# Two ends of a 32-group pipeline: the last group's graphs taken apart, and the setup put ahead of everything

## The chip, the cores and the metric

The kernel runs on one core of a Trainium2 chip. The metric is the device time of one execution in microseconds; lower is better. The core has five engines that run side by side and wait for each other through semaphores: TensorE (PE, matrix products and transposes into PSUM; PEld is its loading of weights), VectorE (DVE), ScalarE (ACT), GpSimd (POOL) and SyncE (SP, which here only issues transfers). ScalarE can issue transfers too, in its own order with its other work.

## What is computed

64 graphs of 256 nodes with 256 features each pass four layers. Each layer is attention over the neighbours that the adjacency matrix allows, a residual and a normalisation.

```python
def reference(x, adj, ...):
    # layer 0: 4 heads, projections Wq Wk Wv Wo, its own layer norm inside
    x = _layernorm(x + _L0_gnn_ref(x, adj, L0_gnn_Wq, ...))
    # layer 1: 8 heads, q = k = v = layer_norm(x); then an MLP
    #          x + gelu(y @ W1 + b1) @ W2 + b2        (256 -> 1024 -> 256)
    x = _layernorm(x + _L1_gnn_ref(x, adj, ..., L1_gnn_W1, L1_gnn_b1, L1_gnn_W2, L1_gnn_b2))
    # layer 2: one head, e[i,j] = leaky_relu(s1[i] + s2[j]), Wh = x @ W
    x = _layernorm(x + _L2_gnn_ref(x, adj, L2_gnn_W, L2_gnn_a))
    # layer 3: one head, scores x * a0 @ x^T, leaky_relu, softmax
    x = _layernorm(x + _L3_gnn_ref(x, adj, ...))
    return x                                          # (64, 256, 256) float32
```

(cut and abridged.)

## The kernel before

Two graphs make a group (G = 2), 512 tokens in four blocks of 128 (TB = 4; QB = 2 blocks per graph). There are 32 groups. Each group is a generator; at each `yield` the others go on, so that the instructions of up to three groups are interleaved. Group 0 begins at step 0, the next one every 15 steps (PACE). TensorE's instructions keep the order in which the program names them.

First the loads, most of them through SyncE:

```python
    setup = act.tile([P, NF, T], F32, name="setup", tag="hT", bufs=1)...   # scratch in hT's place
    first = load_group(0)                                   # x and adj, through SyncE
    wqT = load_rows("L0_gnn_WqT", D, nc.scalar)             # through ScalarE: these four alone
    wkT = load_rows("L0_gnn_WkT", D, nc.scalar)
    bq = load_column(a["L0_gnn_bq"], D, "bq", nc.scalar)
    bk = load_column(a["L0_gnn_bk"], D, "bk", nc.scalar)
    wvT = load_rows("L0_gnn_WvT", D)                        # through SyncE: the rest
    woT = load_rows("L0_gnn_WoT", D)
    ...                                                     # bv, bo, wx, a12, beta0, gamma0, ..., a0
    second = load_group(1)
    w1 = load_rows("L1_gnn_W1", DFF)
    w2 = load_rows("L1_gnn_W2", D)
```

Then the layers. The parts that matter here (cut):

```python
    def project(dst, srcT, w, extra, row=None):
        chunks = w.shape[1]
        for i in range(G):
            pm = ps_m.tile([P, QB, D], F32, name="pm")
            for q in range(QB):
                t = i * QB + q
                for c in range(chunks):
                    matmul(pm[:, q, :], srcT[:, c, t * P:(t + 1) * P], w[:, c, :], ...)
                if row is not None:
                    matmul(pm[:, q, :], onesb, row, start=False, stop=True)
                if chunks > NC:
                    yield
            ...                                             # add the residual

    def layer1(xb, z, mask):
        ...                                                 # attention
        hT = act.tile([P, NF, T], F32, name="hT", bufs=1)
        ...                                                 # W1 and gelu into hT
        yield from project(x2, hT, w2, both, b2m)           # the MLP's second product
        return (yield from renormed(x2))

    def renormed(y, var=None):
        xn = act.tile([P, TB, W], F32, name="xn")
        for i in range(G):
            mv, rstd = stats(y, i)                          # DVE statistics, GpSimd's power
            scaled(xn, y, i, mv, rstd[:, 0])                # DVE
        ...
        return xn

    def values_of(e, v, one, x, rs, var=None):              # e^T v, divided, plus x, renormed
        ...

    def layer2(x, mask):
        xT = transposed(x)                                  # 8 transposes, 2 ScalarE copies
        ...                                                 # wh = x W in 4 blocks, ScalarE copies
        nc.scalar.activation(ex, wh[:, :, D:D + 3], AF.Exp)
        ...                                                 # 4 transposes of ex, 4 DVE products into e
        nc.vector.tensor_tensor(e..., e..., mask..., ALU.mult)
        return (yield from values_of(e, wh, D + 3, x, ...))

    def layer3(g, x, mask):
        for c in range(NC):
            pt = to_psum(x, c)
            nc.scalar.copy(xT[:, c, :], pt)
            nc.scalar.activation(xa[:, c, :], pt, AF.Identity, scale=a0[:, c:c + 1])
        ...                                                 # ps = xT^T xa, 8 products
        nc.scalar.activation(e, ps, AF.Exp, bias=shift)
        nc.scalar.activation(low, ps, AF.Exp, bias=shift, scale=SLOPE)
        nc.vector.tensor_tensor(e, e, low, ALU.max)
        nc.vector.tensor_tensor(e..., e..., mask..., ALU.mult)
        return (yield from values_of(e, x, D, x, r_3[:, g], last[:, g]))

    def group(g):
        x, adj = (first, second)[g] if g < 2 else load_group(g)
        yield
        adjb = io.tile([P, TB, N], BF16, name="adjb", bufs=1)             # one buffer for all groups
        nc.scalar.activation(adjb, adj, AF.Copy, accum_out=there[:, g:g + 1])
        nc.scalar.activation(adj.bitcast(F32), adj, AF.Square, ...)
        yield
        ...                                                 # 8 transposes of adjb, mask on DVE from both
        xb, z = yield from layer0(g, x, mask)
        x = yield from layer1(xb, z, mask)
        x = yield from layer2(x, mask)
        x = yield from layer3(g, x, mask)
        nc.sync.dma_start(out[g * G:(g + 1) * G]..., x[:, :, 0:D])
```

The setup's arithmetic is a generator of its own, `prepare`, whose parts come from step 5 on, between the steps of group 0: `bop` (bo plus bv Wo), three extra columns of `wx` (from L2's W and a), `b2m` (b2 minus beta1 as three bf16 rows, each written by a small transfer from DVE's `part`), and `bounds` (from wsum, the product `ones` x `wsum` on PE and a GpSimd power), which the final flag reads.

Of the kernel before, what the change touches and what calls it, by code (L numbers as in the profile page):

```python
# [8 lines left out]
F32 = mybir.dt.float32  # L9
# [7 lines left out]
P = 128  # L17
N = 256
# [19 lines left out]
PREPARE = 5  # L38
# [357 lines left out]
def usual_input(ctx: ExitStack, tc: tile.TileContext, a: dict, out: bass.AP, flag: bass.AP):  # L396
# [52 lines left out]
    def load_rows(name, cols, queue=nc.sync):  # L449

        src = a[name]
        t = const.tile([P, src.shape[0] // P, cols], F32, name=name)
        queue.dma_start(t, src.rearrange("(c p) f -> p c f", p=P))
        return t

    def load_column(src, n, name, queue=nc.sync):

        t = const.tile([P, n // P], F32, name=name)
        queue.dma_start(t, src.rearrange("(c p) -> p c", p=P))
        return t  # L460

    setup = act.tile([P, NF, T], F32, name="setup", tag="hT", bufs=1).rearrange("p f t -> p (f t)")

    def load_all(src, name, at=None):

        t = const.tile([P, D], F32, name=name) if at is None else setup[:, at:at + D]
        nc.sync.dma_start(t, src.unsqueeze(0).to_broadcast([P, D]))
        return t


    first = load_group(0)
    wqT = load_rows("L0_gnn_WqT", D, nc.scalar)
    wkT = load_rows("L0_gnn_WkT", D, nc.scalar)
    bq = load_column(a["L0_gnn_bq"], D, "bq", nc.scalar)
    bk = load_column(a["L0_gnn_bk"], D, "bk", nc.scalar)
    wvT = load_rows("L0_gnn_WvT", D)
    woT = load_rows("L0_gnn_WoT", D)
    bv = load_column(a["L0_gnn_bv"], D, "bv")
    bo = load_all(a["L0_gnn_bo"], "bo", 0)

    wx = const.tile([P, NC, D + 3], F32, name="wx")
    nc.sync.dma_start(wx[:, :, 0:D], a["L2_gnn_W"].rearrange("(c p) f -> p c f", p=P))
    a12 = setup[:, 768:1280].rearrange("p (s d) -> p s d", s=2)
    nc.sync.dma_start(a12, a["L2_gnn_a"].rearrange("(s f) o -> o s f", s=2).to_broadcast([P, 2, D]))
    beta0 = load_all(a["L0_gnn_beta"], "beta0")
    gamma0 = load_all(a["L0_gnn_gamma"], "gamma0")
    beta1r = load_all(a["L1_gnn_beta1"], "beta1r")
    gamma1r = load_all(a["L1_gnn_gamma1"], "gamma1r", 256)
    b2 = load_all(a["L1_gnn_b2"], "b2", 512)
    gamma1 = load_column(a["L1_gnn_gamma1"], D, "gamma1")  # L490
    beta1 = load_column(a["L1_gnn_beta1"], D, "beta1")
    gamma2 = load_column(a["L1_gnn_gamma2"], D, "gamma2")
    beta2 = load_column(a["L1_gnn_beta2"], D, "beta2")
    b1 = load_column(a["L1_gnn_b1"], DFF, "b1")
    a0 = load_column(a["L3_gnn_a0"], D, "a0")
    second = load_group(1)
    w1 = load_rows("L1_gnn_W1", DFF)
    w2 = load_rows("L1_gnn_W2", D)

    wa1 = const.tile([P, 2, NC], F32, name="wa1")  # L500
    b2m = const.tile([P, D], BF16, name="b2m")
    onesb = const.tile([P, P], BF16, name="onesb")
    bop = const.tile([P, D], F32, name="bop")
    bounds = const.tile([P, 2], F32, name="bounds")

# [49 lines left out]
    def to_psum(src, c):  # L555

        pt = ps_m.tile([P, T], F32, name="pm")
        for t in range(TB):
            transpose(pt[:, t * P:(t + 1) * P], src[:, t, c * P:(c + 1) * P], ident)
        return pt  # L560

    def transposed(src, scale=None, bias=None):

        dst = act.tile([P, NC, T], F32, name="xT")
        for c in range(NC):
            pt = to_psum(src, c)
            if scale is None:
                nc.scalar.copy(dst[:, c, :], pt)
            else:
                nc.scalar.activation(dst[:, c, :], pt, AF.Identity, bias=bias[:, c:c + 1], scale=scale[:, c:c + 1])  # L570
        return dst
# [109 lines left out]
    def project(dst, srcT, w, extra, row=None):  # L681
# [3 lines left out]
        for i in range(G):  # L685
# [76 lines left out]
    def layer1(xb, z, mask):  # L762
# [34 lines left out]
        yield from project(x2, hT, w2, both, b2m)  # L797
        return (yield from renormed(x2))

    def renormed(y, var=None):  # L800
# [3 lines left out]
        for i in range(G):  # L804
            mv, rstd = stats(y, i)
            if var is not None:
                nc.gpsimd.tensor_copy(var[:, i * QB:(i + 1) * QB], mv[:, :, 1])
            scaled(xn, y, i, mv, rstd[:, 0])
# [4 lines left out]
    def values_of(e, v, one, x, rs, var=None):  # L813

        y = act.tile([P, TB, D], F32, name="y")
        for t in range(TB):
# [9 lines left out]
        return (yield from renormed(y, var))  # L826

    def layer2(x, mask):
        xT = transposed(x)
# [5 lines left out]
        for tb in range(TB):  # L835
# [9 lines left out]
        nc.scalar.activation(ex, wh[:, :, D:D + 3], AF.Exp)  # L845
        pt = ps_m.tile([P, G, N], F32, name="pm")
        for t in range(TB):
            transpose(pt[:, t // QB, t % QB * P:(t % QB + 1) * P], ex[:, t, 0:1].to_broadcast([P, P]), ident)
        e = act.tile([P, G, QB, N], F32, name="qT")
        for t in range(TB):  # L850
            i, kc = divmod(t, QB)
            nc.vector.tensor_scalar(e[:, i, kc, :], pt[:, i, :], ex[:, t, 1:2], ex[:, t, 2:3], ALU.mult, ALU.max)
        nc.vector.tensor_tensor(e.rearrange("p g k q -> p (g k q)"), e.rearrange("p g k q -> p (g k q)"),  # L853
                                mask.rearrange("p g k -> p (g k)"), ALU.mult)
        yield
        return (yield from values_of(e, wh, D + 3, x, small.tile([P, TB], F32, name="r")))

    def layer3(g, x, mask):
        xT = act.tile([P, NC, T], F32, name="xT")
        xa = act.tile([P, NC, T], F32, name="z")  # L860
        for c in range(NC):
            pt = to_psum(x, c)
            nc.scalar.copy(xT[:, c, :], pt)
            nc.scalar.activation(xa[:, c, :], pt, AF.Identity, scale=a0[:, c:c + 1])
        yield
        ps = ps_s.tile([P, G, QB, N], F32, name="ps")
        for i in range(G):
            for kc in range(QB):
                for c in range(NC):
# [5 lines left out]
        nc.scalar.activation(e, ps, AF.Exp, bias=shift)  # L875
        nc.scalar.activation(low, ps, AF.Exp, bias=shift, scale=SLOPE)  # L876
        nc.vector.tensor_tensor(e, e, low, ALU.max)  # L877
        nc.vector.tensor_tensor(e.rearrange("p g k q -> p (g k q)"), e.rearrange("p g k q -> p (g k q)"),
                                mask.rearrange("p g k -> p (g k)"), ALU.mult)
        yield  # L880
        yield from rest("e3")
        return (yield from values_of(e, x, D, x, r_3[:, g], last[:, g]))

    def group(g):
        x, adj = (first, second)[g] if g < 2 else load_group(g)
# [18 lines left out]
        x = yield from layer1(xb, z, mask)  # L904
        x = yield from layer2(x, mask)
        x = yield from layer3(g, x, mask)
        nc.sync.dma_start(out[g * G:(g + 1) * G].rearrange("b (q p) d -> p (b q) d", p=P), x[:, :, 0:D])

    def prepare():


        bvr = setup[:, 2560:2816].rearrange("p (c q) -> p c q", c=NC)
        nc.vector.tensor_copy(bvr, bv.unsqueeze(2).to_broadcast([P, NC, P]))
        pm = ps_m.tile([P, D], F32, name="pm")
        for c in range(NC):
            matmul(pm, bvr[:, c, :], woT[:, c, :], start=c == 0, stop=c == NC - 1)
        nc.vector.tensor_tensor(bop, pm, bo, ALU.add)

        yield
        wa = setup[:, 1280:2304].rearrange("p (s c d) -> p s c d", s=2, c=NC)  # L920
        for s in range(2):
            nc.vector.tensor_tensor(wa[:, s], wx[:, :, 0:D], a12[:, s:s + 1, :].to_broadcast([P, NC, D]), ALU.mult)
        nc.vector.tensor_reduce(wa1, wa, AX.X, ALU.add)
        for k, (s, share) in enumerate(((0, SLOPE - 1.0), (1, SLOPE), (1, 1.0))):
            nc.vector.tensor_scalar(wx[:, :, D + k:D + k + 1], wa1[:, s, :].unsqueeze(2), share, None, ALU.mult)

        yield

        nc.gpsimd.memset(onesb, 0.0)
        nc.gpsimd.memset(onesb[0:3, :], 1.0)  # L930
        nc.gpsimd.memset(b2m, 0.0)
        left = setup[:, 2304:2560]
        nc.vector.tensor_tensor(left, b2, beta1r, ALU.subtract)
        part = setup[:, 3328:3456].bitcast(BF16)
        for k in range(3):
            nc.vector.tensor_copy(part, left)
            nc.sync.dma_start(b2m[k:k + 1, :], part[0:1, :])
            if k < 2:
                nc.vector.tensor_tensor(left, left, part, ALU.subtract)

        yield

        sq = setup[:, 2816:3328].rearrange("p (s d) -> p s d", s=2)
        nc.vector.tensor_tensor(sq[:, 0], gamma1r, gamma1r, ALU.mult)
        nc.vector.tensor_tensor(sq[:, 1], beta1r, beta1r, ALU.mult)
        lengths = const.tile([P, 4], F32, name="lengths")
        nc.vector.tensor_reduce(lengths[:, 0:1], sq[:, 0], AX.X, ALU.max)
        nc.vector.tensor_reduce(lengths[:, 1:2], sq[:, 1], AX.X, ALU.add)
        wsq = const.tile([P, 2, NC], F32, name="wsq")
        nc.vector.tensor_tensor(wsq, wa1, wa1, ALU.mult)  # L950
        wsum = const.tile([P, 2], F32, name="wsum")
        nc.vector.tensor_reduce(wsum, wsq, AX.X, ALU.add)
        pm = ps_m.tile([P, 2], F32, name="pm")
        matmul(pm, ones, wsum, start=True, stop=True)
        nc.vector.tensor_copy(lengths[:, 2:4], pm)
# [16 lines left out]
    while waiting or running:  # L972
# [8 lines left out]
        if step >= PREPARE:  # L981
            next(preparing, END)
# [54 lines left out]
```

## Time and profile before

| | before |
|---|---|
| time, median of 3 (lowest, highest) | 2766.12 us (2765.04, 2766.6) |
| span of the profiled execution | 2764.3 us |
| PE busy | 2678.1 us (97%) |
| DVE busy | 1932.5 us (70%) |
| ACT busy | 1294.7 us (47%) |
| POOL busy | 576.8 us (21%) |
| first product or transpose on PE | 10.85 us |
| transfers in the first 35 us | 7.63 MB |
| last normalisation ends | 2756.64 us |

The profile is one execution seen by the hardware profiler. It gives for every engine when each instruction ran and what ended the wait before it. In its lines, L521 and L524 are the helpers through which all of the groups' products and transposes go, so that tiles, not lines, tell them apart: `pm<-v,qT` is a product into PSUM tile pm from v and qT. "x16" is the number of instructions (a float32 product runs as two passes, so 8 products give 16). The granted PE clock is a share of full speed.

### The profile page before, as it was taken

Reading aid. Unit: us, or ns where it says so; the run is one execution under the profiler, and the core shown is the slowest. Engines: PE = TensorE matmul, PEld = TensorE weight load, DVE = VectorE, ACT = ScalarE, POOL = GpSimd, SP = SyncE. Lnnn points to the kernel's source line nnn. Section 1 sums busy time; section 2 is a strip of 40 time slices with the busy share of each in tenths; the row PEclk is TensorE's granted clock in tenths of the full one; section 3 lists DMA queues with packets and bytes.
Section 4 is the critical chain, followed back from the end, with each engine's and each line's share of the span. In section 5 each row is a group of like instructions: output and inputs, shape, how many; then the busy total and the mean of one; then the engine's idle time right before and its main releaser. Section 6 shows DMA issues by size and latency. Waiting matters only on the chain.

```text
span 2764.3 us, 45617 instructions
## 1 busy us (share of the span) xinstructions
PE 2678.1 (97%) x17288; PEld 1842.3 (67%) x17288; DVE 1932.5 (70%) x6346; ACT 1294.7 (47%) x1953; POOL 576.8 (21%) x1138
## 2 busy tenths in 40 slices
PE   6999999999999999999999999999999999999986
PEld 3666666666666767666667666666666666666664
DVE  5667776777676777766777767677767776767754
ACT  3444544544544444544445445445444445444441
POOL 1112121221221221212221222222212212222211
PEclk8999999999999999999999999999999999999998
DMA  4000000000000000000000000000000000000000
GB/s 126 16 8 24 16 24 16 24 16 16 24 21 19 16 24 16 24 16 24 16 24 16 24 16 24 16 20 20 24 16 17 23 16 24 9 16 9 9 8 16
DMA packets 57904, 57.78 MB, mean 21 GB/s; under 512 B 5072, under 2 KB 57296, under 8 KB 57680
## 3 DMA queue, kind: packets, MB, share of 16 engines
q1 hardware_dynamic: 56592, 54.28, 6.4%
q8 instruction: 139, 2.28, 0.3%
q14 instruction: 85, 0.70, 0.1%
q10 hardware_dynamic: 1088, 0.53, 0.1%
HBM read 38.02 MB, written 16.78 MB: 20 GB/s over the span
## 4 chain that ended last, share of the span: by engine, by line
PE 68%; DVE 20%; POOL 8%; issue 2%; ACT 1%; DMA 1%; POOLq 0%; SPq 0%; ACTq 0%; DVEq 0%
PE pm L521 53%; PE ps L521 9%; PE pm L524 6%; POOL rstd L544 6%; DVE xn L552 4%; DVE e L597 3%; DVE st L537 3%; POOL ve L540 2%; DVE z L552 1%; DVE e L591 1%; DVE mv L538 1%; ACT e L589 1%; DVE y L750 1%; DVE xb L756 1%; DVE xb L552 1%
## 5 line engine op out<-in xcount | busy, mean ns | idle before, releaser
L589 ACT ACTIVATE e<-ps 128x1024 f32<-128x1024 f32 x384 | 372.2, 1021 | 356.5 <-PE ps L521 353.3
L521 PE MATMUL pm<-L_gnn_W,hT 128*128 128x256 f32 x2048 | 463.2, 379 | 0.0
L521 PE MATMUL pm<-xT,L_gnn_W 128*128 128x512 f32 x1024 | 450.6, 593 | 0.0
L521 PEld LDWEIGHTS pm<-L_gnn_W,hT 128*128 128x128 f32 x2048 | 383.9, 190 | 63.2 <-issue 15.1
L597 DVE SCALAR_TENSOR_TENSOR e<-e,mask 128x256 f32<-128x256 f32 x1024 | 399.3, 454 | 29.1 <-ACT e L589 29.1
L794 ACT ACTIVATE hT<-pm,b 128x512 f32<-128x512 f32 x256 | 175.9, 687 | 477.5 <-PE pm L521 477.5
L540 POOL TENSOR_SCALAR ve<-mv 128x2 f32<-128x2 f32 x384 | 93.1, 243 | 1315.5 <-DVE mv L538 1121.7
L521 PEld LDWEIGHTS pm<-xT,L_gnn_W 128*128 128x128 f32 x1024 | 192.5, 190 | 216.5 <-issue 214.2
L537 DVE BATCH_NORM_STATS2 st<-y 128x6 f32<-128x256 f32 x768 | 300.4, 410 | 5.6
L544 POOL TENSOR_TENSOR rstd<-ve,mhalf 128x2 f32<-128x2 f32 (+1 forms) x384 | 297.9, 776 | 26.6
L552 DVE TENSOR_SCALAR xn<-y,mv,rstd 128x256 f32<-128x256 f32 x384 | 163.5, 472 | 127.2 <-POOL rstd L544 127.2
L877 DVE TENSOR_TENSOR qT<-qT,kT 128x1024 f32<-128x1024 f32 x32 | 39.2, 1226 | 195.1 <-ACT kT L876 195.1
L521 PE MATMUL pm<-e,z 128*32 128x256 f32 x2048 | 149.2, 385 | 3.7 <-DVE e L597 2.9
L521 PE MATMUL pm<-e,v 128*32 128x256 f32 x2048 | 135.5, 382 | 16.9 <-DVE e L591 16.9
L591 DVE TENSOR_TENSOR e<-e,mask 128x1024 f32<-128x1024 f32 x128 | 148.3, 1220 | 0.5 <-ACT e L589 0.5
L521 PE MATMUL ps<-xT 32*128 32x256 f32 x2048 | 147.8, 402 | 0.0
L780 POOL TENSOR_TENSOR both<-y,xb 128x512 f32<-128x512 f32 x64 | 81.7, 1277 | 314.6 <-DVE y L779 314.6
L718 POOL TENSOR_TENSOR x<-x,beta 128x1024 f32<-128x1024 f32 x32 | 75.5, 2359 | 334.9 <-PE pm L524 334.9
L570 ACT ACTIVATE xT<-pm,beta,gamma 128x512 f32<-128x512 f32 x128 | 92.9, 773 | 103.9 <-PE pm L524 103.6
L521 PE MATMUL ps<-qT,kT 64*128 64x256 f32 x1024 | 128.0, 389 | 0.3 <-ACT e L589 0.3
L538 DVE BATCH_NORM_AGGREGATE mv<-st 128x2 f32<-128x6 f32 x768 | 121.6, 171 | 3.0
L521 PE MATMUL pm<-v,qT 128*128 128x260 f32 x512 | 120.3, 389 | 3.3 <-DVE qT L853 3.3
(144 smaller groups left out, 4321.1 us busy)
## 6 DMA issues: line engine op xcount, KB each, us to landing
x<-in_x SPq DMA_DIRECT2D x32, 512.0 KB, 3.8
adj<-in_adj SPq DMA_DIRECT2D x32, 512.0 KB, 3.8
out<-xn SPq DMA_DIRECT2D x32, 512.0 KB, 2.9
L_gnn_W<-in_L_gnn_W SPq DMA_DIRECT2D x2, 1024.0 KB, 8.6
L_gnn_WqT<-in_L_gnn_WqT ACTq DMA_DIRECT2D x1, 256.0 KB, 4.9
L_gnn_WkT<-in_L_gnn_WkT ACTq DMA_DIRECT2D x1, 256.0 KB, 6.8
L_gnn_WvT<-in_L_gnn_WvT SPq DMA_DIRECT2D x1, 256.0 KB, 7.5
L_gnn_WoT<-in_L_gnn_WoT SPq DMA_DIRECT2D x1, 256.0 KB, 7.8
```

Of the source, the lines that this page charges most:

```text
L521: in_order(nc.tensor.matmul(*args, **kw))
L524: in_order(nc.tensor.transpose(*args))
L537: nc.vector.bn_stats(st[:, q, :], src[:, t, 0:D])
L538: nc.vector.bn_aggr(mv[:, q, :], st[:, q, :])
L540: nc.gpsimd.tensor_scalar(ve[:, 0], mv[:, :, 1], EPS, None, ALU.add)
L544: nc.gpsimd.tensor_tensor(rstd, ve, mhalf[:, 0:k * QB].rearrange("p (k t) -> p k t", k=k), ALU.pow)
L552: nc.vector.tensor_scalar(dst[:, t, 0:D], src[:, t, 0:D], mv[:, q, 0:1], rstd[:, q:q + 1], ALU.subtract, ALU.mult)
L570: nc.scalar.activation(dst[:, c, :], pt, AF.Identity, bias=bias[:, c:c + 1], scale=scale[:, c:c + 1])
L589: nc.scalar.activation(e, ps, AF.Exp, scale=scale)
L591: nc.vector.tensor_tensor(e, e, mask.unsqueeze(1).to_broadcast([P, 2, QB * N]), ALU.mult)
L597: nc.vector.scalar_tensor_tensor(e[:, h, k], e[:, h, k], 1.0, mask[:, k], ALU.mult, ALU.mult, accum_out=sums[:, kc, c, j:j + 1])
L794: nc.scalar.activation(hT[:, f, :], pm, AF.Gelu, bias=b1[:, f:f + 1])
```

## The change

It has two parts. For the last group alone, from the MLP's second product on, the two graphs go separately: each is its own generator, the second one two turns behind the first, so that one graph's waits may be filled with the other's work. And the beginning has another form: all weights come through ScalarE, x and adj of the first groups through SyncE, and the setup's arithmetic stands ahead of the groups instead of between their steps.

```diff
-    first = load_group(0)
-    wqT = load_rows("L0_gnn_WqT", D, nc.scalar)
-    wkT = load_rows("L0_gnn_WkT", D, nc.scalar)
...
+    wqT = load_rows("L0_gnn_WqT", D)              # load_rows, load_column and load_all
+    wkT = load_rows("L0_gnn_WkT", D)              # all use nc.scalar.dma_start now
+    wvT = load_rows("L0_gnn_WvT", D)
+    woT = load_rows("L0_gnn_WoT", D)
...                                                # bq bk bv bo gamma0 beta0 gamma1 beta1 ...
+    w1 = load_rows("L1_gnn_W1", DFF)
+    b1 = load_column(a["L1_gnn_b1"], DFF, "b1")
+    w2 = load_rows("L1_gnn_W2", D)
+    b2 = load_all(a["L1_gnn_b2"], "b2", "xn")
+    wx = const.tile([P, NC, D + 3], F32, name="wx")
+    nc.scalar.dma_start(wx[:, :, 0:D], ...)
+    a12 = act.tile([P, 2, D], F32, name="a12", tag="z")
+    nc.scalar.dma_start(a12, ...)
+    for s in range(2):
+        nc.vector.tensor_tensor(wa[:, s], wx[:, :, 0:D], a12[:, s:s + 1, :]..., ALU.mult)
+    nc.vector.tensor_reduce(wa1, wa, AX.X, ALU.add)
...
+    for k in range(3):
+        nc.vector.tensor_copy(part, rest)
+        nc.sync.dma_start(b2m[k:k + 1, :], part[0:1, :])
...                                                # bop, squares, lengths, wsum
+    nc.tensor.matmul(pm, ones, wsum, start=True, stop=True)
+    nc.vector.tensor_copy(lengths[:, 2:4], pm)
+    nc.gpsimd.tensor_tensor(roots, lengths, half, ALU.pow)
...                                                # longest, bounds
-    def project(dst, srcT, w, extra, row=None):
+    def project(dst, srcT, w, extra, row=None, gs=ALL):
...                                                # the same gs in to_psum, transposed, renormed,
...                                                # values_of, layer2, layer3
     def group(g):
-        x, adj = (first, second)[g] if g < 2 else load_group(g)
+        x, adj = load_group(g)
...
-        x = yield from layer1(xb, z, mask)
-        x = yield from layer2(x, mask)
-        x = yield from layer3(g, x, mask)
-        nc.sync.dma_start(out[g * G:(g + 1) * G]..., x[:, :, 0:D])
-
-    def prepare():
...
+        y, hT, both = yield from layer1(xb, z, mask)
+
+        def others(gs):
+            yield from project(y, hT, w2, both, b2m, gs)
+            x = yield from renormed(y, gs)
+            x = yield from layer2(x, mask, gs)
+            x = yield from layer3(g, x, mask, gs)
+            i, j = g * G + gs[0], g * G + gs[-1] + 1
+            nc.sync.dma_start(out[i:j]..., x[:, gs[0] * QB:(gs[-1] + 1) * QB, 0:D])
+
+        if g < B // G - 1:
+            yield from others(ALL)
+            return
+
+        parts = [others((i,)) for i in ALL]
+        turn = 0
+        while parts:
+            for r in parts[:turn // QB + 1]:
+                if next(r, END) == END:
+                    parts.remove(r)
+            turn += 1
+            yield
```

(cut at "..."; comments in the diff are added here.)

## The prediction

> **What bounds the kernel now.** I read the page first, then the busy time by stretches, then the timeline of the two ends. The stretches (columns: busy time with instruction counts of PE, PEld, DVE, ACT and POOL; granted PE clock; DMA share; GB/s):
>
> ```profile
> 0.00:40.00 40.00, 27.09 (x194) 16.87 (x195) 18.22 (x44) 16.85 (x27) 5.07 (x19) 1.00 0.70 191
> 40.00:70.00 30.00, 15.78 (x92) 10.18 (x93) 20.62 (x72) 9.26 (x13) 7.35 (x11) 0.72 0.11 36
> 70.00:2660.00 2590.00, 2560.26 (x16711) 1761.08 (x16709) 1846.05 (x6095) 1244.28 (x1874) 549.24 (x1072) 1.00 0.06 18
> 2660.00:2712.00 52.00, 47.78 (x201) 34.43 (x202) 24.46 (x65) 17.12 (x26) 8.01 (x16) 0.97 0.03 11
> 2712.00:2764.00 52.00, 27.16 (x93) 19.76 (x91) 23.16 (x74) 7.14 (x13) 7.13 (x20) 0.76 0.06 22
> ```
>
> Between 70 and 2660 us PE is busy 99% of the time, at full clock. The compiled order of the changed kernel has the same instructions in the same order there on every engine, so that stretch is worth zero. What can change is when it starts (the first 70 us) and what follows it (the last 52 us, where PE is half idle). A later start moves everything behind it one for one, because a full PE can't catch up.
>
> The start of before, from the timeline (start, duration, engine, line, operation):
>
> ```profile
> 8.33 1.06 ACT L888 ACTIVATE adjb<-adj 128x1024 bf16<-128x1024 int32 x1 [3.87 <-DMA adj<-in_adj]
> 10.85 1.01 PE L524 MATMUL pm<-identb,adjb 128*128 128x128 bf16 x8 [10.85 <-ACT adj L889]
> 13.12 3.44 DVE L922 TENSOR_TENSOR setup<-wx,setup 128x512 f32<-128x512 f32 x2
> 13.60 0.59 ACT L568 COPY xT<-pm 128x512 f32<-128x512 f32 x1 [0.27 <-PE pm L524]
> 25.84 2.00 PE L521 MATMUL ps<-qT,kT 64*128 64x256 f32 x16
> 27.61 0.29 DVE L936 CAST setup<-setup 128x256 bf16<-128x256 f32 x1 [6.90 <-DMA b2m<-setup]
> ```
>
> The first group waits only for its own adjacency (landed at 8.3 us); the setup arithmetic fits into gaps. First scores start at 25.84 us, my reference point. All starting loads together keep the DMA engines busy to about 30 us.
>
> The end of before, from its timeline:
>
> ```profile
> 2723.59 6.51 PE L521 MATMUL pm<-v,qT 128*128 128x260 f32 x16 [3.33 <-DVE qT L853]
> 2736.26 5.37 PE L521 MATMUL ps<-z,xT 128*128 128x256 f32 x16 [0.41 <-ACT z L864]
> 2741.66 1.11 ACT L875 ACTIVATE qT<-ps,shift 128x1024 f32<-128x1024 f32 x1 [4.39 <-PE ps L521]
> 2746.45 5.29 PE L521 MATMUL pm<-xn,qT 128*128 128x257 f32 x16 [4.82 <-DVE qT L878]
> ```
>
> and the last normalisation in the chain of waits (start, duration, what):
>
> ```profile
> 2755.91 0.73 DVE xn L552 x2
> ```
>
> One dependent chain for both graphs: every stage waits for the one before, the engines take turns, and PE gets 0.76 of its clock. It ends with that normalisation at 2756.64; the rest to 2764.3 is the output's landing, the flag and the program's end.
>
> **What the Trainium skill says.** (1) "DMA: Bandwidth & Descriptors", section "Issuing engines are not separate DMA queues": transfers issued from SyncE and ScalarE share the same 16 DMA engines, and a second issuer only saves issue time. The trace agrees: with both issuing, the first 10 us moved 227 GB/s at a DMA share of 0.86. So the second queue doesn't shorten the loading. (2) "SBUF — State Buffer", section "SBUF: two separate sides", on the shared port pair: VectorE operations with two SBUF inputs and GpSimd operations lock each other out. The trace agrees: one of the two L922 products took 689 ns, the other 2835 ns, when GpSimd's 2.36 us addition ran at 13.65. The changed order has GpSimd idle there, so I count 0.69 us each. (3) "TensorE: Matmul & The Clock Gate", Part 1: an idle window of some 3.4 us halves PE's clock. The trace agrees at both ends (0.50 in 50 to 60 us, 0.66 in 2720 to 2740), but not for the first 10 us, idle at 1.00.
>
> **The change, part by part: the start.** In the compiled order, ScalarE issues 23 loads before its first activation; SyncE has only x and adj of the first two groups ahead of the b2m copies. VectorE does the whole setup before the first mask, and PE's second product of all is the one of wsum, ahead of the first transposes. So nothing of group 0 moves on PE before a12, the last large load, has landed and VectorE is through.
>
> *When a12 lands.* Before moved 7.63 MB by about 30 us. Up to a12 it is now 6.56 MB: four loads of 0.524, four weights of 0.262, W1 and W2 with 2.10, wx and a12 0.52, six broadcast rows 0.79. The 1.05 MB less (adj of groups 2 and 3) is 3 us at 350 GB/s, and some gaps between issues vanish: 26.5 us, within 24 to 29. ScalarE is past its last issue at about 18 us by my count of issue times (0.5 us each) and reused completion semaphores, so it isn't the last wait.
>
> *VectorE to wsum.* Durations of before: L922 2 x 0.69, bop 0.42, L923 1.21, cast 0.28, wx 0.29, rest 0.41, squares 2 x 0.41, lengths 2 x 0.40, wsq and wsum 0.30, sum 5.9: 32.4 us. The second cast needs the first b2m copy read; that took 8.7 us in before behind W1 and W2 on SyncE's queue. Now that queue is nearly empty, b2 lands ahead of wx and a12, and I expect no wait.
>
> *To the first scores.* wsum on PE 0.4, its copy 0.15 and hops: 33.3. GpSimd's roots 1.03: 34.4. Seven small VectorE operations 1.04: 35.5. The mask 1.23: 36.8. Only then group 1's adjb on ScalarE (there is one adjb buffer), 1.06 + 0.19: 38.1. In the compiled order the second xT copy of group 0 stands behind that: 0.59, so 38.7. In before that copy ended at 14.2 and the scores began 11.6 later; without bop's product between Q and K (0.87) that is 10.8. Scores at 49.5, that is 23.7 later. After that before lost about 1.3 us to setup operations standing ahead of score masks (mask 2 ready at 29, done at 31.2) which no longer occurs: 22.4. A cold PE after 30 idle us may cost some: I add 1. **Start: +23.4 us.**
>
> **The end.** The PE order of the changed kernel: graph 0's four transposes, its wx; graph 1's transposes, its wx; ex of 0, values of 0, ex of 1, values of 1; transposes and ps of 0, then of 1; last values of 0, then of 1. W2's products and group 30's last values keep their places, so the split begins to act at 2713.2. Halving durations of before:
> - wx of graph 0 starts at 2714.1 (before: 2715.1), graph 1's ends at 2719.0. VectorE is busy with group 30 to 2719.95, so graph 0's mask is done at 2721.6 (before, both: 2723.5).
> - Values of 0 at the slow clock, 3.2: 2724.8. Graph 1's ex stands behind them in PE's order; its mask is done at 2728.0, its values at 2731.3.
> - Transposes of 0 after that, ScalarE's four copies of 0.4: 2733.5; ps 2735.2; exponentials 2736.6; then the copies of graph 1, its ps at 2739.6.
> - Values of 0 2739.6 to 2742.2; graph 1's exponentials to 2741, its mask 2743.6, its values to 2746.4; y, statistics, GpSimd's 1.0, xn: 2750.0.
>
> Against 2756.65 that is 6.65 us. PE's strict order makes graph 1 wait behind graph 0 twice, which is why half-size stages don't bring more. **End: -6.7 us**, within -3 to -11.
>
> **Sum.** 2766.1 + 23.4 - 6.7 = 2782.8, rounded to 2783.
>
> **Rivals.** (a) The later start is hidden, as loads overlap with setup anyway. For: ScalarE's casts and the transfers do overlap. Against: PE did 27 us of work in the first 40 us, which now comes later, and the middle has 1% of slack. With the start lost only to 10 us the end's gain nearly covers it: about 2769. (b) The end gains more, because interleaving two graphs keeps PE warm. v, ps and last values take 6.5 + 5.4 + 5.3 us, against 3.6 to 3.7 each for the groups of 16 at full clock in the timeline near 2677, 2695 and 2709; warm throughout and without stalls the end would be 11 to 14 us shorter: about 2777. Against: gaps of 2 to 3 us remain in my schedule. (c) The first b2m copy queues behind the loads as in before (8.7 us): second cast only at 34 or later instead of 30, start +27: about 2787. Against: the queue is now another. (d) Waits for lanes of completion semaphores starve the DMA engines between 10 and 15 us, when small loads are alone: a12 at 29 to 30, about 2786.
>
> **Range and chances.** The start's error is mainly a12's landing (2.5 us to either side) and the clock; the end's some 3 us. Together some 7 us: 2775 to 2791. The two per cent are 55 us either way; neither end has so much to win or lose. Faster 0.01, same 0.97, slower 0.02.
>
> **What would show it.** First transposes on PE at 33 us, having waited for VectorE's wsum; the first L922-like product waiting for a12 at about 26.5; the two products 0.69 us each; first scores near 49.5; PE full again from about 93; from there to 2713 the same length as before; the last xn some 6.7 us sooner relative to group 30's last values. Wrong would be: first scores under 42 (a12 earlier, or the setup off the path), or a tail shorter by over 11 us or not at all.

## Result: where the changed kernel's time lies

| | before | after |
|---|---|---|
| time, median of 4 (lowest, highest) | 2765.6 us (2764.9, 2766.6) | 2776.6 us (2775.2, 2779.2) |
| ratio, 95% interval | | 1.0041 (1.0023 to 1.0058) |
| span of the profiled execution | 2764.3 us | 2777.4 us |
| first scores of group 0 on PE | 25.84 us | 48.03 us |
| group 30's last values start | 2709.74 us | 2731.19 us |
| last normalisation ends | 2756.64 us | 2770.22 us |

The change costs 11.1 us by the medians, within 2%. The profiled execution of after is the slowest of the four, 13.1 us over that of before. The table splits it: the start costs 21.45 us (2731.19 - 2709.74), the end gives back 7.87 (46.90 us from group 30's last values to the last normalisation before, 39.03 after), which makes 13.6; the flag and the program's end took 0.5 less. Group 30's last values on PE, in before and in after, and the last normalisation of after:

```profile
2709.74 3.63 PE L521 MATMUL pm<-xn,qT 128*128 128x257 f32 x16
```

```profile
2731.19 3.63 PE L567 MATMUL pm<-xn,qT 128*128 128x257 f32 x16
...
2769.49 0.73 DVE L598 TENSOR_SCALAR xn<-y,mv,rstd 128x256 f32<-128x256 f32 x2 [0.40 <-POOL rstd L590]
```

Two stretches of after, with the columns of the prediction's first fence (busy time with counts of PE, PEld, DVE, ACT and POOL; clock; DMA share; GB/s):

```profile
90.00:2670.00 2580.00, 2551.49 (x16635) 1755.79 (x16637) 1836.33 (x6048) 1240.83 (x1868) 547.02 (x1064) 1.00 0.06 18
...
2725.00:2777.00 52.00, 31.82 (x133) 24.46 (x131) 28.02 (x90) 8.21 (x22) 8.51 (x26) 0.87 0.07 22
```

The middle is as full of PE work as before (98.9% busy). The last 52 us hold more PE work than before (31.82 against 27.16 us) at a higher clock (0.87 against 0.76), but as the end is shorter they reach some 8 us further back into the full stretch. Over the same work, from group 30's last values to the last normalisation, PE was busy 25.24 of 39.03 us at a clock of 0.91, against 28.86 of 46.90 us at 0.82 in before.

The start of after, from its timeline:

```profile
20.13 0.48 ACTq L492 DMA_DIRECT2D a<-in_L_gnn_a  x1
...
24.09 0.43 DVE L510 TENSOR_TENSOR rest<-b,beta1r 128x256 f32<-128x256 f32 x1 [21.93 <-DMA b<-in_L_gnn_b]
...
25.48 1.29 DVE L495 TENSOR_TENSOR wa<-wx,a 128x512 f32<-128x512 f32 x2
...
30.91 0.56 PE L540 MATMUL pm<-wsum,ones 128*128 128x2 f32 x2 [4.06 <-DVE wsum L538]
...
31.32 1.01 PE L570 MATMUL pm<-identb,adjb 128*128 128x128 bf16 x8
...
33.72 1.21 DVE L955 SCALAR_TENSOR_TENSOR mask<-pm,adjb 128x1024 bf16<-128x1024 bf16 x1
...
34.97 1.06 ACT L944 ACTIVATE adjb<-adj 128x1024 bf16<-128x1024 int32 x1 [1.16 <-DVE mask L955]
...
36.03 0.57 ACT L623 COPY xT<-pm 128x512 f32<-128x512 f32 x1
...
36.65 4.57 PE L567 MATMUL pm<-xT,L_gnn_WqT 128*128 128x512 f32 x6 [0.71 <-ACT xT L623]
...
48.03 2.00 PE L567 MATMUL ps<-qT,kT 64*128 64x256 f32 x16
```

The chain reads downwards: the load of a (a12 in the code) is issued at 20.13 and takes 5.3 us to land; VectorE, which waited for b2 until 24.09 and worked on it until 25.37, takes a at 25.48; PE waits for wsum; group 0's transposes stand behind that product; the mask follows the bounds; group 1's adjb waits for the mask; and group 0's second xT copy stands behind that adjb on ScalarE. In before the transposes ran at 10.85.

The end of after, PE's timeline:

```profile
2743.18 3.50 PE L567 MATMUL pm<-v,qT 128*128 128x260 f32 x8 [2.20 <-DVE qT L909]
2746.48 0.60 PE L570 MATMUL pm<-ident,ex 128*128 128x128 f32 x2
2749.71 3.21 PE L567 MATMUL pm<-v,qT 128*128 128x260 f32 x8 [2.64 <-DVE mv L584]
...
2754.19 2.20 PE L567 MATMUL ps<-z,xT 128*128 128x256 f32 x8 [0.41 <-ACT z L920]
...
2758.39 2.20 PE L567 MATMUL ps<-z,xT 128*128 128x256 f32 x8 [1.56 <-ACT z L920]
2760.43 1.90 PE L567 MATMUL pm<-xn,qT 128*128 128x257 f32 x8
2763.92 1.97 PE L567 MATMUL pm<-xn,qT 128*128 128x257 f32 x8 [1.60 <-DVE qT L935]
```

Layer 3's passes are near full pace again (1.90 us for 8; 5.29 for 16 in before), but the two groups of layer 2's values still run slow (3.50 and 3.21 us for 8), and graph 1's exponent transposes stand behind graph 0's values.

### The profile page after: what moved, and what is told of

The parts are those of the page before. It is cut to its first block, busy times and chain, and to the rows that moved or that the text cites. A ratio compares the mean times of both kernels' runs of the same rounds, so it can differ in the third digit from the quotient of the medians.

```text
span 2777.4 us, 45647 instructions
## 1 busy us (share of the span) xinstructions
PE 2677.1 (96%) x17288; PEld 1840.5 (66%) x17288; DVE 1932.8 (70%) x6349; ACT 1296.9 (47%) x1962; POOL 578.8 (21%) x1142
## 4 chain that ended last, share of the span: by engine, by line
PE 68%; DVE 20%; POOL 8%; issue 2%; ACT 1%; DMA 1%; ACTq 0%; POOLq 0%; DVEq 0%
PE pm L567 53%; PE ps L567 9%; PE pm L570 6%; POOL rstd L590 6%; DVE xn L598 4%; DVE e L652 3%; DVE st L583 3%; POOL ve L586 2%; DVE z L598 1%; DVE mv L584 1%; DVE e L646 1%; ACT e L644 1%; DVE y L805 1%; DVE xb L811 1%; DVE xb L598 1%
## 5 line engine op out<-in xcount | busy, mean ns | idle before, releaser
L934 DVE TENSOR_TENSOR qT<-qT,kT 128x1024 f32<-128x1024 f32 (+1 forms) x33 | 39.3, 1192 | 187.3 <-ACT kT L933 187.3
```

## Experiments

Each time is a median, with its difference to the runs of before on the same chip. "Old" and "new" are the parts as in before and after. The edits are shown cut and abridged.

### The end alone

```diff
-    (new start)                     # loads through ScalarE, arithmetic ahead
+    (start of before)               # the last group split, as in after
```

> The start of the kernel before, the last group's graphs taken apart as in the changed kernel. Theory (the two parts add up; the end gains what the last normalisations showed, 13.6 against 21.4 us later): 7.9 us less than before, about 2758, the last normalisation near 2749. Rival (the end's gain is an effect of the later start, or lies within the spread): 2766, no change.

Measured: 2757.98 us, -7.9, ratio 0.9971 (0.9959 to 0.9982). From group 30's last values to the last normalisation 39.00 us, as in after (39.03). The split is worth what it gains inside the change, and alone it is faster than both kernels.

### The start alone

```diff
-        if g < B // G - 1:          # every group but the last goes whole
+        if g < B // G:              # all groups go whole; the start is new
```

> The start of the changed kernel, the last group as before. Theory: the start alone costs 20.8 to 21.4 us, so about 2787. Rival (the start costs only what the whole change costs): 2777.

Measured: 2787.74 us, +21.8, ratio 1.0078 (1.0061 to 1.0095), first scores at 48.87 us. The two parts add to 13.9 us; the whole change measured 11.1 with an interval of 6.4 to 16.0 (its ratio's bounds by 2765.6), and 13.6 in its profiled execution. So nothing shows that they touch each other; an effect of a few microseconds can't be told from the spread.

### The start's two halves

First the arithmetic ahead of group 0, with the loads in before's order and queues:

```diff
     # old: first = load_group(0), the early weights on ScalarE, the rest on SyncE
-    (prepare's parts between group 0's steps)
+    (wa, b2m, bop, wsum, bounds ahead of the first group)
```

> Loads in the order and on the queues of before, only the setup's arithmetic ahead of the groups; last group as before. Theory (wait for a12, then the arithmetic, then wsum on PE): a12 lands at 12.7 us as in before, wsum is on PE near 19, the mask is made near 22, first scores near 34 instead of 25.8, less 1.4 us for score masks that no longer wait: 7 us more than before, about 2773. Rival (the order of the loads and ScalarE's issuing are all of the cost): within 1 us of before, 2766.

Measured: 2772.03 us, +6.1, ratio 1.0022 (1.0013 to 1.0031). Its timeline:

```profile
12.83 1.29 DVE L497 TENSOR_TENSOR wa<-wx,a 128x512 f32<-128x512 f32 x2 [10.67 <-DMA a<-in_L_gnn_a]
...
20.67 1.01 PE L569 MATMUL pm<-identb,adjb 128*128 128x128 bf16 x8
...
34.40 2.00 PE L566 MATMUL ps<-qT,kT 64*128 64x256 f32 x16
```

With the load of a in its old place VectorE has it at 12.83 us instead of 25.48, and the transposes wait only until 20.67. Scores come 8.6 us late, as expected to half a microsecond.

Then the loads as in after, with the arithmetic between group 0's steps:

```diff
-    first = load_group(0); wqT ... on ScalarE; wvT ... second, w1, w2 on SyncE
+    first = load_group(0); second = load_group(1); all weights on ScalarE, in after's order
     (prepare's parts between group 0's steps, as in before)
```

> Loads as in the changed kernel (weights through ScalarE in its order, x and adj through SyncE), the arithmetic between the steps as in before; last group as before. Theory: group 0's adjb comes at 22.4 us as ScalarE issues first; PE doesn't wait for wsum, but VectorE's compiled order has the products with a12 and the second b2m cast ahead of the mask, so mask near 30, first scores near 44: 16 to 18 us more than before, about 2783. Rival (the arithmetic ahead is all of the cost): 2766. Second rival (ScalarE's late casts alone, 14 us): 2780 with first scores near 40.

Measured: 2783.61 us, +17.7, ratio 1.0068 (1.0051 to 1.0085). Its timeline:

```profile
24.64 1.03 PE L523 MATMUL pm<-identb,adjb 128*128 128x128 bf16 x8 [24.64 <-ACT adjb L887]
...
29.88 1.21 DVE L898 SCALAR_TENSOR_TENSOR mask<-pm,adjb 128x1024 bf16<-128x1024 bf16 x1
...
31.13 1.06 ACT L887 ACTIVATE adjb<-adj 128x1024 bf16<-128x1024 int32 x1 [3.99 <-DVE mask L898]
```

Group 0's adjacency isn't what is late. ScalarE, which must turn it into adjb, is still issuing loads: the last of its 23 was issued at 21.66 us here (one of them alone held it for 4.05 us), and adjb's activation began at 23.43, behind a table load of 1.28. Then the mask comes only at 29.88, behind the a products, their sum and the second b2m cast on VectorE, and ScalarE waits for it. First scores began at 44.73, as expected. So the larger share of the cost is that loads stand ahead of computing on ScalarE and the load of a far back among them; the two weren't tried apart. The arithmetic ahead delays the first scores by another 4.1 us (48.87 - 44.73), where alone it delayed them by 8.6, so about half of it lies in the same wait. In the times it is 4.1 us (21.8 - 17.7) against 6.1 alone, two figures that the intervals don't separate.

### The bounds out of the first group's way

```diff
     (new start, old end)
-    (squares, lengths, wsum, ones x wsum, roots, bounds ahead of group 0)
+    (the same after the last group, ahead of the flag; gamma1r keeps a buffer of its own)
```

> The changed start whole (all loads through ScalarE, arithmetic ahead of group 0) with the old end, but the computation of the two bounds (squares, sums, the product with ones, roots) is moved behind the last group; nothing else needs it before. Theory (what holds PE up in the changed start is VectorE's chain behind the attention vectors, and the bounds are only its last link): PE's first transposes no longer wait for the product with ones, the mask comes some 5 us sooner (near 29 instead of 34), the scores of group 0 near 43 instead of 48.9, and the time some 5 us under the new start alone (2787.7): about 2782, with a microsecond lost at the end for the bounds at most. Rival (the start is bound by the loads' arrival and by GpSimd, the bounds are beside it): scores at 48 to 49, time 2786 to 2788.

Measured: 2779.90 us, +14.6, ratio 1.0049 (1.0031 to 1.0067): 7.3 us less than the new start alone, each against its own runs of before. Its timeline:

```profile
28.64 1.06 PE L545 MATMUL pm<-identb,adjb 128*128 128x128 bf16 x8
...
31.09 1.22 DVE L930 SCALAR_TENSOR_TENSOR mask<-pm,adjb 128x1024 bf16<-128x1024 bf16 x1
31.23 3.70 PE L542 MATMUL pm<-xT,L_gnn_WqT 128*128 128x512 f32 x8
...
41.75 2.00 PE L542 MATMUL ps<-qT,kT 64*128 64x256 f32 x16
```

Scores at 41.75, 7.1 us sooner than in the new start alone, although the a products began 1.4 us later here (27.45 against 26.07). More than the 5 expected came back because both xT copies now go ahead of group 1's adjb and Q's 8 passes run at full pace in one go (3.70 us; in the new start alone 2.07 for two, a wait, then 4.83 for six). The pace may be luck, as it differs from run to run even with the same start (last section). The bounds are needed only by the flag.

### The two graphs in the same turn

```diff
-            for r in parts[:turn // QB + 1]:      # the second graph two turns behind
+            for r in list(parts):                 # both in every turn   (old start)
```

> The old start; the last group's two graphs go apart, but without an offset: each step of graph 1 follows the same step of graph 0. Theory (the end gains because one graph's VectorE and ScalarE steps lie beside the other's products, and in the changed kernel graph 1's exponent transposes sit behind graph 0's values, which held PE 2.2 us): the gain stays and grows a little, some 2 us under the split with the offset (2758.0): about 2756. Rival (it is the offset by one turn that makes the two graphs fill each other's waits): without it the two graphs wait at the same places, and the gain of 7.9 mostly goes: 2763 to 2766.

Measured: 2757.06 us, -8.3, ratio 0.9966 (0.9953 to 0.9979); 38.15 us from group 30's last values to the last normalisation. That is 0.9 us better than with the offset in the medians, which the intervals don't separate. The offset isn't what makes the gain.

### One graph after the other

```diff
-            for r in parts[:turn // QB + 1]:
+            for r in parts[:1]:                   # graph 1 starts when graph 0 is through
```

> The old start; the last group's two graphs go apart, and graph 1 begins its second MLP product only when graph 0 has gone through all its steps, so that nothing of one lies beside the other's waits. Theory (the gain of the split is overlap): the gain is lost; graph 0's chain of some 22 us from its second product on, then 7.5 us of graph 1's product, then its chain of 22 and the flag's 12: the end near 2770 (2766 to 2776), above the kernel before. Rival (the gain comes from steps of half the size alone): at or under the split with the offset, 2755 to 2760.

Measured: 2784.31 us, +19.0, ratio 1.0067 (1.0049 to 1.0085). Half-size steps without the other graph beside them lose all of the gain and 19 us more. I had expected some 14 us less. PE's clock fell further than assumed, as the last stretch's window shows; how much of the 14 us that makes was not taken apart:

```profile
2750.00:2781.00 31.00, 13.24 (x32) 8.89 (x32) 10.08 (x31) 3.19 (x8) 1.96 (x5) 0.60 0.03 10
```

In this run 8 passes of layer 2's values took 3.84 us for graph 0 and 3.47 for graph 1, and those of layer 3's scores 3.78 for each.

### PE kept busy in the old end

Nothing is left out here; products that nobody reads are added.

```diff
+    def fill(n):                                  # only in the last group's layers 2 and 3
+        for k in range(n if filler else 0):
+            matmul(spare[:, 0], identb, mask[:, 0], start=True, stop=True)    # 128x512, bf16
...
+        fill(12 if one > D else 17)               # ahead of layer 2's, of layer 3's values
+        fill(4 if t == 0 else 7)                  # ahead of each graph's transposes in layer 3
```

> The kernel before, whole, with products whose result nobody reads put into PE's order in the last group's layers 2 and 3, in front of the steps that PE waits for: 12 ahead of layer 2's values, 4 and 7 ahead of the transposes of its two graphs, 17 ahead of layer 3's values (identity by mask, 128x512). No result changes. Theory A (PE runs slow at the end because it idles: 6.51, 5.37 and 5.29 us for 16 passes that take 3.63 us at full clock in the middle): the fillers keep the granted clock up, the three groups come down to about 3.7 us, and the time falls by about 6 us, to near 2760. Then part of the split's gain can be a warmer PE. Theory B (the pace at the end is set by something else, or the clock does not answer to such products): the three groups stay over 5 us and the time stays at 2765 to 2768; the split's gain is overlap alone.

Measured: 2759.92 us, -5.4, ratio 0.9980 (0.9972 to 0.9989). PE's timeline, then its window (2720 to 2730 us had clock 0.66 in before):

```profile
2718.98 2.54 PE L521 MATMUL ps<-mask,identb 128*128 128x512 bf16 x11
2722.25 3.77 PE L521 MATMUL pm<-v,qT 128*128 128x260 f32 x16 [0.74 <-DVE qT L862]
...
2741.69 3.71 PE L521 MATMUL pm<-xn,qT 128*128 128x257 f32 x16 [1.15 <-DVE qT L887]
```

```profile
2720.00:2730.00 10.00, 8.28 (x37) 4.72 (x34) 6.92 (x22) 0.00 (x0) 1.87 (x5) 1.00 0.11 38
```

The old end ran at half its possible pace on PE because PE idled: 6.51 us becomes 3.77, 5.29 becomes 3.71, at a clock of 1.00 in the window shown; layer 3's scores, 5.37 us before, took 3.99 and a wait of 0.36 between their passes. This answers to the Trainium skill, "TensorE: Matmul & The Clock Gate", section "Why this matters for your kernels", which asks for no idle gaps of PE above some 3 us: the waits left here are 1.15 us and less. The split in the same turn shows that waits below 3 us can be too long as well: none of its waits near layer 2's values was over 1.91 us, but those 16 passes took 5.30 us, with a clock of 0.83 in 2720 to 2730 us. There the measurement is stricter than the page.

### Both, twice

The split in the same turn, with such products in its gaps (8, 5, 6 and 9 of them):

```diff
-        ps = ps_s.tile([P, G, QB, N], F32, name="ps")
+        ps = shared if filler else ps_s.tile([P, G, QB, N], F32, name="ps")   # one for both graphs
+        fill(8 if one > D else 9)                 # ahead of graph 0's values
+            fill(5 if gs[0] == 0 else 6)          # ahead of the transposes of layer 3
```

> The old start, the last group's two graphs apart in the same turn (as in the run of 2757.1), and products whose result nobody reads in the gaps that PE has there: 8 ahead of layer 2's values, 5 and 6 ahead of the transposes of the two graphs, 9 ahead of layer 3's values. If the split's gain and PE's clock are two separate gains, they add: 8.3 and 5.4 us, to near 2752. If the split gains in part because it already keeps PE warmer (its three groups took 5.30, 5.03 and 4.02 us there, where 3.7 is to be had), the fillers can only take back what is left of that, 1.6, 1.3 and 0.3 us: near 2754. If the split's gain was wholly PE's clock, nothing is left: 2757.

Measured: 2757.64 us, -8.6, ratio 0.9968 (0.9956 to 0.9980): nothing over the split alone in the time (37.01 against 38.15 us in the end itself), as if PE's pace no longer mattered. But the trace shows that this run hindered itself:

```profile
2735.96 1.99 PE L521 MATMUL ps<-z,xT 128*128 128x256 f32 x8 [1.36 <-ACT kT L897]
2738.01 1.89 PE L521 MATMUL ps<-mask,identb 128*128 128x512 bf16 x8
2739.73 3.63 PE L521 MATMUL pm<-xn,qT 128*128 128x257 f32 x16
```

Graph 1's scores waited for graph 0's exponentials, because I had put both into one PSUM tile, and the added products ran on after 2737.36, when graph 0's weights were ready. So I gave each graph a tile, let the added products write into the half that its graph doesn't use, and put 4 instead of 9 ahead of layer 3's values:

```diff
-        ps = shared if filler else ...
+        ps = filler[1 + gs[0]] if filler else ...
-        fill(8 if one > D else 9)
+        fill(8) if one > D else fill(4, 0)
```

> As the run before (2757.6), whose trace shows that it hindered itself: both graphs' scores of layer 3 lay in one PSUM tile, so that graph 1's scores waited 1.36 us for graph 0's exponentials, and the 8 products in front of layer 3's values ran 1.4 to 2.4 us past the moment when the first graph's weights were ready. Here each graph has its own tile, the products in the gaps go into the half that its graph doesn't use, and only 4 stand in front of layer 3's values. If the split's gain and PE's clock add, if only in part: 2 to 3 us under the split in one turn (2757.1), 2754 to 2755. If the split has taken PE's slow passes off the path already, so that nothing is left for a faster PE: 2756 to 2758.

Measured: 2752.49 us, -12.7, ratio 0.9953 (0.9940 to 0.9967), better than any kernel here and 24 us under the changed one by the medians of the two comparisons. Its PE timeline:

```profile
2721.32 3.77 PE L521 MATMUL pm<-v,qT 128*128 128x260 f32 x16 [0.18 <-DVE qT L873]
...
2730.38 3.62 PE L521 MATMUL ps<-z,xT 128*128 128x256 f32 x16
2733.84 1.03 PE L521 MATMUL ps<-mask,identb 128*128 128x512 bf16 x4
2735.17 4.02 PE L521 MATMUL pm<-xn,qT 128*128 128x257 f32 x16 [0.31 <-DVE qT L899]
```

The two gains add for the most part: by the medians, 8.3 for the split and 5.4 for the clock make 13.7, of which 12.7 came. The table gives the end alone: 8.75 and 5.31 make 14.06, of which 11.62 came; the other 1.1 us of the 12.7 lie ahead of the end, as group 30's last values began at 2708.64 in the profiled execution (2709.74 in before). What the shared tile and the 9 products cost each isn't known, as both were changed at once. The end in one measure, from group 30's last values to the last normalisation:

| old end | + products in the gaps | split, offset | split, same turn | split, one shared tile + products | split, two tiles + products |
|---|---|---|---|---|---|
| 46.90 us | 41.59 us | 39.00 us | 38.15 us | 37.01 us | 35.28 us |

## Why the prediction was right, and where it was off

The forecast was 2783 us in a range of 2775 to 2791, 16.9 us above before; measured were 2776.6, 11.1 above. The middle, the place of the loss and the sign of each part held; both parts were mis-sized in the same direction, the start by 2.0 us and the end by 1.2. Of the other 2.6 us between 16.9 and 11.1, 0.5 are the flag and the program's end; most of the rest is that the medians lie closer together than the two profiled executions.

**The start: +23.4 predicted.** By the trace +21.45, in the run of the start alone +21.8.

| step | predicted, us | after, us |
|---|---|---|
| VectorE takes a | 26.5 | 25.48 |
| wsum done | 32.4 | 30.76 |
| roots done | 34.4 | 32.85 |
| mask | 35.5 to 36.8 | 33.72 to 34.93 |
| second xT copy ends | 38.7 | 36.60 |
| first scores | 49.5 | 48.03 |

Every link of the chain was there in the order named, but its head is shared: I had VectorE wait for a alone, and it waited for b2 until 24.09 and then hardly at all, as its work on b2 ended (25.37) when a landed (20.13 + 5.3). That head was set 1.0 us too late: I worked the landing out of bytes at 350 GB/s. VectorE's stretch was 0.6 too long (5.28 us instead of 5.9; small operations overlap at their ends, two squares of 0.42 us began at 29.09 and 29.43), and the steps from wsum to the second copy 0.5 (5.84 instead of 6.3). The allowance for a cold PE was 1 us; from that copy to the scores it was 0.6 more than the 10.8 taken from before, all of it in Q's passes (4.45 us from the copy's end to K's first pass, where before without bop's product had 3.80). What was to be recovered later (1.3 us) measured 1.4: group 0's first zs transposes ran at 57.58 against 36.82. That is 20.76 later; the last 0.7 up to 21.45 came in the middle, from there to group 30's last values (2673.61 us against 2672.92), and is no more than chance: with the start of before, group 30's last values began between 2708.40 and 2711.64 us in six profiled executions.

I had counted ScalarE's last issue at 18 us and dismissed it. It was at 20.65, after one issue that took 3.10 us. In after adjb's lateness stayed hidden behind the arithmetic, but in the run with only the loads moved it is what the transposes waited for, at 24.64.

**The end: -6.7 predicted.** Measured -7.9, in the trace of the whole change and as the median of the split alone. Taken from group 30's last values, layer 2's values of the two graphs began within 0.3 us of the schedule (2743.18 and 2749.71 less 21.45: 2721.7 and 2728.3, against 2721.6 and 2728.0). From there on the passes of layer 3 ran faster than halves of before's slow ones: scores 2.20 us where half of 5.37 is 2.7, last values 1.90 and 1.97 where I had 2.6. With that, and with 0.7 less between graph 1's exponentials and its weights (1.9 us where I had 2.6), graph 1's last values ended 2.0 us ahead of the schedule (2744.4 against 2746.4); the statistics and normalisation behind them took 4.3 us where I had 3.6, so that 1.2 are left.

**Rivals.** (a), a hidden start, fell: the runs with after's loads and the old end are 14.6 to 21.8 us above before. (b), a warmer PE, was underrated. Its mechanism is real and worth 5.4 us by itself; in the changed kernel it is used only in part, since layer 2's values still ran at 0.40 to 0.44 us a pass against 0.24. Split and warmth together reach 12.7, within the 11 to 14 that I had named for an end warm throughout. (c) fell: the first b2m copy was issued at 24.99 and the second cast ran at 28.35 without waiting. (d) fell by its figure, as the load of a had landed by 25.48 and not at 29 to 30, though little moved between 13 and 17 us (159 GB/s at a DMA share of 0.82; 325 at 1.01 between 17 and 25).

## What to carry to other kernels

Where one engine is full in the middle, price a change by its two ends alone, and follow each end link by link through the compiled order of every engine: a side computation ahead of the first group costs its latency even when each engine has time for it, and an engine that issues loads can't compute meanwhile (ScalarE here, up to its last issue at 20.65 us). In an end that is one dependent chain, splitting it into two halves side by side and keeping PE's clock up with products that nobody reads are two gains that add for the most part, if the added products don't outlast the gap and neither half has to wait for a tile that the other still reads.

## What was not expected

PE's first large products run at half pace, though the clock column shows 1.00 there. In after, Q's six passes took 4.57 us and K's eight, right behind them, 3.60; the weight loads for Q's passes stand 0.85 us apart up to 40.19 us and 0.43 from there. In before Q's eight took 4.77 us. Only in the run with the bounds moved did Q run at full pace from its first pass (3.70 us for 8), after 4.39 us of PE work in the 4.45 since 26.78. How much work it takes isn't settled: in after 5.0 us of it (30.91 to 35.94) and a wait of 0.71 went before Q's slow passes, and with only the arithmetic ahead 4.97 without a wait (18.24 to 23.21) before 4.37 us for Q's eight. With the same start, Q's eight took from 3.89 to 5.34 us in seven profiled executions. So the clock column doesn't tell whether a kernel's first products are slow; the length of one pass does.

In the best run, VectorE and GpSimd make 15.0 of the last 24.2 us of the chain up to the last normalisation, in steps of at most 0.74 us, and PE 6.8. A further gain at the end would have to come from there; that wasn't tried.
